# Message passing on a graph: 43 instead of 18 double groups of edges brought column by column or row by row, on ScalarE, VectorE and SyncE

## The chip, the cores and the metric

The kernel runs on one core of a Trainium2 chip. The metric is the device time of one execution in microseconds (us), lower is better; a median of several executions is compared. The core's engines each run their own instructions in order: TensorE (PE in the profile; its weight loads are PEld), VectorE (DVE), ScalarE (ACT), GpSimd (POOL) and SyncE (SP). They wait for each other through semaphores.

## The reference, cut to what matters

There are 12,500 nodes with 128 features, and 400,000 edges sorted by their target `dst`. Each edge has a random source `src` and 32 attributes.

```
h = max(layernorm(x), 0)
m = relu(concat(h[src], h[dst], edge_attr) @ w1 + b1) @ w2 + b2   # 288 -> 128 -> 128
agg = segment_sum(m, dst, 12500)
gi, gh = agg @ w_ih + b_ih, h @ w_hh + b_hh
r, z = sigmoid(i_r + h_r), sigmoid(i_z + h_z);  n = tanh(i_n + r * h_n)
out = x + (1 - z) * n + z * h
```

The part that cannot be a plain matrix product is `h[src]`: for every edge, the row of a random node.

## The kernel before

**Tables.** A first part normalises all nodes. It keeps `h` transposed in SBUF (`hT_all`, 128 features by 12,500 nodes, L60) and writes `A = h @ w1[0:128]` to DRAM (L118, L319), one row of 512 bytes for each node. So what an edge needs of its source is either the row `A[src]`, or the column `hT_all[:, src]`, which TensorE then multiplies by `w1a`.

**Tiling.** 128 edges are a tile and 8 tiles a double group (`PAIR`), 1,024 edges; there are 391 double groups (`NP`), numbered k. A double group is worked off in two units u = 2k and u = 2k+1 of four tiles each.

**The usual way of a double group.** GpSimd issues 8 indirect DMAs (`gather`, L135 to L146), each fetching 128 rows of `A` into a buffer `G`. There are `GBUFS` = 8 such buffers of 4 KB per partition, and 4 more that are in use only at the beginning (`EARLY`; the first ten double groups gather raw `x` rows, as `A` isn't ready yet). TensorE makes the other part of the layer in PSUM (`pre`, L582): a one-hot of the targets and the edge attributes, `L`, times `RW`, whose upper rows are the window's node rows. VectorE adds `G` (`add`, L605), ScalarE applies the ReLU (`relu`, L617), and TensorE sums the result by target with a second one-hot `OH` (`seg`, L625). VectorE takes the sums from PSUM (`take`, L638, whose count column ScalarE casts).

**By hand.** 18 double groups, listed in `order` (L83 to L91), aren't gathered. `one_by_one` (L762) copies, for each of the 1,024 edges, one column of `hT_all` (128 partitions by 4 bytes) into a tile `HE`: ScalarE by a copy (L775) for 10 double groups, VectorE by a `tensor_reduce` over one element (L777) for 8. The place of the column is in a register. 32 of them are loaded at a time by a register load (`LOAD`, L768), from a row of the tile `at`, which a DMA (L759) filled with node numbers and L880 turned into byte places. For such a double group `pre` adds 8 products with `w1a` (L601), `add` does nothing, and `relu` reads PSUM.

**The order of the work.** The program is written out by hand: Tile's scheduler is off (L58), and each engine takes its instructions in the order in which the loop over u (L862) issues them. In unit u stand, in this order: the requests of gathers whose buffer is coming free (`gathers`, L814); on even u, for every second double group, the loads of `L` and `Ld` on SyncE (`fetch`, L477: three DMAs); `run_jobs(u, 0)`; on even u `take(k-1)`; `stages(u)`; `run_jobs(u, 1)`, and on even u `window(k+3)` (VectorE copies 64 columns to `hw`, TensorE multiplies them, `oh`); `run_jobs(u, 2)`; `seg(u)`; `run_jobs(u, 3)`, and on even u `window_rows(k+3)` (VectorE adds `b1b` to `oh`, L524); a step of the node update. `stages(u)` holds on even u the one-hots for double group k+3 (`onehot_T` L489, `onehot` L526), then `pre(u+3)`, `add(u+2)`, `relu(u+2)`.

`run_jobs` (L795) spreads each by-hand job evenly over its units and their four phases, in steps of 4 edges. Jobs begin at unit 2*`JOBS0` = 32; a job ends 4 units before its double group's first unit, and the next of the same engine begins there. For 14 double groups at a time a `node` block (L646) does the gated update: a burst of small products on TensorE (L665, L670), carried over by VectorE (L650, L652), then four gates, each a step of its own, and the result to DRAM (L725).

GpSimd runs ahead of the others as far as free buffers let it; SyncE as far as `L`'s three buffers let it: a `fetch` stands in the program 2 units ahead of the use of what it loads, and its buffer was given back 4 units before it.

Of the kernel before, what the change touches and what calls it, by code (L numbers as in the profile page):

```python
# [8 lines left out]
F32 = mybir.dt.float32  # L9
F16 = mybir.dt.float16  # L10
I32 = mybir.dt.int32
U8 = mybir.dt.uint8
BF16 = mybir.dt.bfloat16
ET = mybir.EngineType
AF = mybir.ActivationFunctionType
ALU = mybir.AluOpType
AX = mybir.AxisListType

N, E, D, DE = 12500, 400000, 128, 32
T = E // 128  # L20

GRP = 4
PAIR = 2 * GRP
# [14 lines left out]
NFULL = N // 128  # L38
BAT = (4,) + (8,) * 11 + (NFULL - 92, 1)
RAW = 10  # L40
GBUFS = 8
EARLY = 4
PLACE = 20
CH = PLACE * PAIR
LOAD = 32
STEP = {"act": 4, "dve": 4}
SPREAD = {"act": 10, "dve": 8}
NR = 12672

H_AT = 16512  # L50
HOLD = -2


@with_exitstack
def tile_gnn(ctx: ExitStack, tc: tile.TileContext, x, src, srcT, dstT, dstP, eaT, eaP, w1, b1, w2T, b2,
             wih, bih, whh, bhh, out):
    nc = tc.nc
    ctx.enter_context(tc.manual_schedule())  # L58
    const = ctx.enter_context(tc.tile_pool(name="const", bufs=1))
    hT_all = const.tile([128, N], F32, name="hT_all")  # L60
    h_bytes = hT_all.bitcast(U8)
    gp = ctx.enter_context(tc.tile_pool(name="gp", bufs=GBUFS))
    p2 = ctx.enter_context(tc.tile_pool(name="p2", bufs=2))
# [7 lines left out]
    def tiles(k):  # L71
        return (0 if k == 0 else SUP0 + (k - 1) * PAIR, SUP0 + k * PAIR)
# [7 lines left out]

    JOBS0 = 2 * EARLY + GBUFS

    mode, order = {}, {m: [] for m in SPREAD}  # L83
    for m, n in SPREAD.items():
        lo = JOBS0 + 15
        for i in range(n):
            k = lo + int((i + 0.5) * (NP - 2 - lo) / n)
# [30 lines left out]
    A = dram.tile([N, D], F32, name="A")  # L118
# [3 lines left out]
    G = {}  # L122

    def early_pair(k):
        return k < EARLY or EARLY + GBUFS <= k < 2 * EARLY + GBUFS

    taker, rings = {}, {True: [], False: []}
    for k in range(NP):
        if k not in mode:
            ring = rings[early_pair(k)]  # L130
            size = EARLY if early_pair(k) else GBUFS
            taker[k] = ring[-size] if len(ring) >= size else -1
# [75 lines left out]
    with tc.tile_pool(name="pp", bufs=3) as pp:  # L208
# [50 lines left out]
        rows = const.tile([1, 6 * D + D], F32, name="rows")  # L259
# [18 lines left out]
        def chunk(q):  # L278
            b, c = chunks[q]
            i0, n = bats[b]  # L280
            return b, i0, c, min(n, c + 4), PB(b), (i0 + c) * 128
# [3 lines left out]
        for q in range(NC + 3):  # L285
            if q < NC:
                b, i0, c, e, P, n0 = chunk(q)
# [3 lines left out]
            if 1 <= q <= NC:  # L291
                b, i0, c, e, P, n0 = chunk(q - 1)
# [6 lines left out]
            if q >= 3:  # L299
                b, i0, c, e, P, n0 = chunk(q - 3)  # L300
# [4 lines left out]
            if q < NC:  # L305
                b, i0, c, e, P, n0 = chunk(q)
# [4 lines left out]
            if 1 <= q <= NC:  # L311
                b, i0, c, e, P, n0 = chunk(q - 1)
# [3 lines left out]
            if q >= 3:  # L316
                b, i0, c, e, P, n0 = chunk(q - 3)
                if e == bats[b][1]:
                    nc.sync.dma_start(nodes(A, i0, e, P), asb[b][:P, :e, :])  # L319
            if 2 <= q <= NC + 1:  # L320
                b, i0, c, e, P, n0 = chunk(q - 2)
                pas[q - 2] = ps2.tile([128, GRP, D], F32, name="pre")
                for j in range(c, e):
                    nc.tensor.matmul(pas[q - 2][:P, j - c, :], columns(b, j, j + 1)[:, 0, :],
                                     w1a, start=True, stop=True)
        for b0, b1, n in ((0, 1, BAT[0]), (1, 12, 8), (12, 13, BAT[12])):
            i0 = sum(BAT[:b0])
            for b in range(b0, b1):
                i = i0 + (b - b0) * n
# [32 lines left out]
    for a in range(2):  # L362
        s = slice(V * a, V * (a + 1))
        nc.vector.tensor_scalar(node_of[s, :], base_b[s, :, a], place_c[s, :], float(-V * a),
                                op0=ALU.add, op1=ALU.add)
# [109 lines left out]
    hand = {}  # L475
# [13 lines left out]
    def onehot_T(k):  # L489
        if k >= NP:  # L490
            return
        c = slice((k % QP) * 512, (k % QP + 1) * 512)
        nc.vector.tensor_scalar(Ls[k // QP][:2 * V, c], Ds[k // QP][:, c], node_of[:, k:k + 1],  # L493
                                None, op0=ALU.is_equal)
# [31 lines left out]
    def onehot(k):  # L526
        if k >= NP:
            return
        t0, t1 = tiles(k)
        OH[k] = OHB[k % len(OHB)]  # L530
        for a in range(2) if k == 0 else (None,):
            if a is None:
                o, s = OH[k].rearrange("p j a v -> p a j v"), slice(t0, t1)
                d = dloc[:, s].rearrange("p (a j) -> p a j", a=2)[:, :, :, None]
                shape = [128, 2, GRP, V]
                i = iota[:, None, None, :]
            else:
                e = min(t1, (a + 1) * GRP)
                o, d = OH[k][:, :e - a * GRP, a, :], dloc[:, a * GRP:e, None]
                shape = [128, e - a * GRP, V]  # L540
                i = iota[:, None, :]
            nc.vector.tensor_tensor(o, d.to_broadcast(shape), i.to_broadcast(shape),  # L542
                                    op=ALU.is_equal)
# [9 lines left out]
    def raw_h(u):  # L553
        if u < 2 * RAW:
            for i, s in enumerate(slots(u)):
                relu_norm(unit(u)[:, s, :], unit(u)[:, s, :], HE[u][:, i, :])

    def raw_stats(u):
        if u < 2 * RAW:
            l = slots(u)  # L560
            HE[u] = bn_sqrt(p2, bn(p2, lambda j: unit(u)[:, l[j], :], 128, len(l)), 128, len(l))

    def raw_fin(u):
        if u < 2 * RAW:
            n = len(slots(u))
            st = p2.tile([128, GRP, 2], F32, name="st_raw", bufs=4)
            bn_fin(p2, st[:, :n, :], HE[u], 128, n)
            HE[u] = st

    def raw_turn(u):  # L570
        if u < 2 * RAW:
            l = slots(u)
            pt = ps1.tile([128, 512], F32, name="misc")
            for i, s in enumerate(l):
                nc.tensor.transpose(pt[:, i * 128:(i + 1) * 128], unit(u)[:, s, :], ident)
            hT = p3.tile([128, 512], F32, name="hTe", bufs=2)
            nc.vector.tensor_copy(hT[:, :len(l) * 128], pt[:, :len(l) * 128])
            HE[u] = hT
# [171 lines left out]

    pj = []
    late = ExitStack()
    by_hand = order["act"] + order["dve"]
    NJ = len(by_hand)
    at = const.tile([NJ, PAIR * 128], I32, name="at")

    def job_indices(r):
# [2 lines left out]
            "(o e) -> o e", o=1))  # L760

    def one_by_one(m, k):  # L762
        et = {"act": ET.Activation, "dve": ET.DVE}[m]
        r = by_hand.index(k)
        hand[k] = pj[0].tile([128, PAIR * 128], F32, name=f"HE_{m}")
        he = hand[k].bitcast(U8)
        for e0 in range(0, PAIR * 128, LOAD):
            _, vals = nc.values_load_multi_w_load_instructions(  # L768
                at[r:r + 1, e0:e0 + LOAD], engines=[et], min_val=H_AT,
                max_val=H_AT + 4 * (N - 1),  # L770
                skip_runtime_bounds_check_because="src holds numbers of nodes")
            for i, v in enumerate(vals):
                e = e0 + i
                if m == "act":
                    nc.scalar.copy(he[:, e * 4:e * 4 + 4], h_bytes[:, bass.ds(v - H_AT, 4)])  # L775
                else:
                    nc.vector.tensor_reduce(he[:, e * 4:e * 4 + 4],  # L777
                                            h_bytes[:, bass.ds(v - H_AT, 4), None],
                                            AX.X, ALU.max)
                if i % STEP[m] == STEP[m] - 1:  # L780
                    yield

# [2 lines left out]
    for m, kl in order.items():  # L785
        start = 2 * JOBS0
        for k in kl:
            end = 2 * k - 4
            jobs.setdefault(start, []).append((m, k, end - start))
            start = end  # L790
    live = {}

    PH = 4
# [1 line left out]
    def run_jobs(u, phase):  # L795
# [3 lines left out]
        if phase == 0:  # L799
            for m, k, span in jobs.get(u, ()):  # L800
                live[m] = [one_by_one(m, k), u, span, PAIR * 128 // STEP[m], 0]
        for m, job in list(live.items()):
# [28 lines left out]
    def stages(u):  # L831
        if u + 7 >= 0:
            raw_stats(u + 7)
        if u + 6 >= 0:
            raw_fin(u + 6)
            raw_h(u + 6)
        if u % 2 == 0:
            onehot_T(u // 2 + 3)
            onehot(u // 2 + 3)
        if u + 4 >= 0:  # L840
            raw_turn(u + 4)
        if u + 3 >= 0:
            pre(u + 3)
        if u + 2 >= 0:
            add(u + 2)
            relu(u + 2)
# [15 lines left out]
    for u in range(NU):  # L862
        k, h = divmod(u, 2)
        gathers(u)
        if h == 0:
            if k % QP == 0:
                fetch(k // QP + 2)
            if k % BP == 0 and k:
                nodes_left.append([node(k // BP - 1), 0])
            if k % PLACE == 1:  # L870
                indices(k // PLACE + 2)
            if k % PLACE == 5:
                place(k // PLACE + 1)
                dst_tile(k // PLACE + 2)
            if k == NP - 20:
                check_windows()
        for r in range(2 * u, min(2 * u + 2, NJ)):
            job_indices(r)
        if u == 2 * JOBS0 - 2:
            nc.vector.tensor_scalar(at, at, 4.0, float(H_AT), op0=ALU.mult, op1=ALU.add)  # L880

        def other(phase):
            run_jobs(u, phase)
            if h == 0 and phase == 1:
                window(k + 3)
            if h == 0 and phase == 3:
                window_rows(k + 3)
            if phase == 3:
                step(nodes_left)

        other(0)
        if h == 0:
            take(k - 1)
        stages(u)
        other(1)
        other(2)
        seg(u)
        if u == 0:
            node_setup()
        other(3)  # L900
# [105 lines left out]
    f = nc.values_load(flag[0:1, 0:1], min_val=0, max_val=1)  # L1006
# [67 lines left out]
```

## Time and profile before

| | us |
|---|---|
| median of 3 runs (3842.6 to 3846.54) | 3845.28 |
| the profiled execution, whole | 3851.33 |
| its span, first to last instruction | 3849.6 |
| POOL busy in the span | 2895.7 (75%) |
| PE busy | 2660.6 (69%) |
| DVE busy | 2007.8 (52%) |
| ACT busy | 1650.1 (43%) |

In the profile an instruction is named by its line, its engine and the tiles that it writes and reads (`G<-A,src_i`). Of a group of like instructions the page gives the number, the time busy, the mean of one in ns, and the idle time of the engine just ahead of them with what ended it: another engine's instruction, a DMA that landed, or "issue", where the engine waited for nothing that the profile shows. Register loads aren't counted as busy; their time shows as idle time that "issue" ended. "SPq" is SyncE's instruction stream. PEclk is the clock granted to TensorE, as a share of full speed. A view of windows gives the busy time of the engines, and the number of instructions, in a stretch of the span.

### The profile page before, as it was taken

What the parts mean: (1) busy time and instruction counts of PE and PEld (TensorE: products, weight loads), DVE (VectorE), ACT (ScalarE), POOL (GpSimd) and SP (SyncE); (2) the same over time, 40 slices, a digit from 0 to 9 for tenths busy, and PEclk for the clock granted to TensorE, in tenths of its full rate; (3) what the DMA queues carried; (4) which work ended last, traced back from release to release, by engine and by line L of the source; (5) the groups of instructions that cost most, each with busy time, mean ns of one, the idle gap of its engine ahead of it and who ended that gap; (6) DMA issues with size and microseconds to landing.
All of it is one profiled execution on the core that took longest, in us unless ns stands there. A gap on an engine that the chain in (4) does not pass through costs nothing. (4 is left out here: it accounts for less than half of the span.)

```text
span 3849.6 us, 62154 instructions
## 1 busy us (share of the span) xinstructions
PE 2660.6 (69%) x13274; PEld 1624.1 (42%) x13274; DVE 2007.8 (52%) x12309; ACT 1650.1 (43%) x11720; POOL 2895.7 (75%) x2989
## 2 busy tenths in 40 slices
PE   6688766766775675776777577666667766775776
PEld 6554443443443443443444344433434443443443
DVE  7766655544545444554555455455545545544432
ACT  5446544444444444443544444444444444444311
POOL 7777777777777777777777777777777777777774
PEclk9888777777777777776777787687867777777776
DMA  6343333333333333333333333333333333333331
GB/s 202 87 99 93 85 91 84 77 87 82 88 82 87 82 84 85 84 86 79 90 84 83 81 88 87 77 92 78 89 80 89 77 87 82 89 80 85 88 81 38
DMA packets 151695, 333.68 MB, mean 87 GB/s; under 512 B 62088, under 2 KB 68019, under 8 KB 151317
## 3 DMA queue, kind: packets, MB, share of 16 engines
q0 software_dynamic: 95392, 195.55, 20.1%
q1 hardware_dynamic: 55781, 134.06, 13.5%
q8 instruction: 110, 1.80, 0.2%
q14 instruction: 268, 2.20, 0.2%
q10 hardware_dynamic: 144, 0.07, 0.0%
HBM read 315.60 MB, written 13.84 MB: 86 GB/s over the span
## 5 line engine op out<-in xcount | busy, mean ns | idle before, releaser
L144 POOL DMA_INDIRECT G<-A,src_i x2904 | 2821.9, 972 | 886.8 <-issue 837.3
L590 PE MATMUL pre<-RW,L 128*128 128x256 f32 x3128 | 1164.7, 505 | 120.4 <-DVE G L615 107.5
L775 ACT COPY HE_act<-hT_all 128x4 uint8 x10240 | 1055.5, 188 | 380.8 <-issue 378.9
L621 ACT ACTIVATE RB<-G 128x512 f32<-128x512 f32 x726 | 456.9, 629 | 1409.2 <-DVE G L615 1099.0
L615 DVE TENSOR_TENSOR G<-pre,G 128x512 f32<-128x512 f32 x726 | 499.8, 688 | 890.4 <-DMA G<-A,src_i 876.2
L515 PE MATMUL oh<-w1b,hw 128*64 128x128 f32 x782 | 217.1, 370 | 1019.8 <-DVE hw L512 1014.0
L590 PEld LDWEIGHTS pre<-RW,L 128*128 128x128 f32 x3128 | 696.7, 246 | 435.2 <-issue 311.3
L777 DVE TENSOR_REDUCE HE_dve<-hT_all 128x4 uint8 x8192 | 641.3, 148 | 359.8 <-issue 354.2
L634 PE MATMUL seg<-RB,OH 128*32 128x129 f32 x6250 | 657.4, 346 | 6.0 <-ACT dcol L643 4.4
L515 PEld LDWEIGHTS oh<-w1b,hw 128*64 128x64 f32 x782 | 92.6, 168 | 1184.2 <-DVE hw L512 1154.0
L634 PEld LDWEIGHTS seg<-RB,OH 128*32 128x32 f32 x6250 | 356.3, 133 | 256.6 <-issue 139.9
L524 DVE TENSOR_TENSOR RW<-oh,b1b 32x128 f32<-32x128 f32 x782 | 218.9, 280 | 171.8 <-PE oh L515 164.8
L642 DVE COPY sums<-seg 64x128 f32<-64x128 f32 x391 | 108.5, 278 | 211.0 <-PE seg L634 207.1
L493 DVE TENSOR_SCALAR L<-Ld,node_of 64x512 f32<-64x512 int32 x391 | 193.9, 496 | 0.1
L643 ACT CAST dcol<-seg 64x1 f16<-64x1 f32 x391 | 59.6, 152 | 261.2 <-DVE sums L642 259.0
L665 PEld LDWEIGHTS nd<-spot,sums 64*128 64x128 f32 x782 | 164.4, 321 | 13.8 <-issue 13.8
L665 PE MATMUL nd<-spot,sums 64*128 64x40 f32 x782 | 168.5, 404 | 0.0
L542 DVE TENSOR_TENSOR OH<-dloc,iota 128x256 f32<-128x256 f16 (+1 forms) x392 | 160.0, 408 | 0.0
L629 PE MATMUL seg<-zrow 1*64 1x129 bf16 x391 | 107.1, 274 | 0.0
L512 DVE COPY hw<-hT_all 128x64 f32 x391 | 85.3, 218 | 18.2 <-issue 7.0
L144 POOL DMA_INDIRECT G<-in_x,src_i x77 | 72.8, 946 | 24.9 <-issue 22.8
L629 PEld LDWEIGHTS <-zrow 1*64 1x64 bf16 x391 | 43.6, 111 | 97.4 <-issue 97.4
(147 smaller groups left out, 1366.4 us busy)
## 6 DMA issues: line engine op xcount, KB each, us to landing
L<-in_eaP SPq DMA_DIRECT2D x195, 256.0 KB
Ld<-in_dstP SPq DMA_DIRECT2D x390, 128.0 KB
G<-A,src_i POOLq DMA_INDIRECT x2904
xb<-in_x SPq DMA_DIRECT2D x28, 256.0 KB
out<-xb SPq DMA_DIRECT2D x28, 256.0 KB
xs<-in_x SPq DMA_DIRECT2D x11, 512.0 KB
A<-asb SPq DMA_DIRECT2D x11, 512.0 KB
src_i<-in_srcT SPq DMA_DIRECT2D x19, 80.0 KB
```

Source lines behind the costliest of these rows:

```text
L144: nc.gpsimd.indirect_dma_start(out=G[k][:, j, a, :], out_offset=None, in_=table, in_offset=bass.IndirectOffsetOnAxis(ap=src_i[c][:, i:i + ...
L493: nc.vector.tensor_scalar(Ls[k // QP][:2 * V, c], Ds[k // QP][:, c], node_of[:, k:k + 1], None, op0=ALU.is_equal)
L515: nc.tensor.matmul(PB_[k][:2 * V, :D], hw.rearrange("p a v -> p (a v)"), w1b, start=True, stop=True)
L524: nc.vector.tensor_tensor(RW[k % 4][s, a, :], pm[s, :D], b1b[s, :], op=ALU.add)
L542: nc.vector.tensor_tensor(o, d.to_broadcast(shape), i.to_broadcast(shape), op=ALU.is_equal)
L590: nc.tensor.matmul(PP[u][:, 2 * i:2 * i + 2, :], Ls[k // QP][:, c0:c0 + 128], RW[k % 4], start=True, stop=not raw)
L615: nc.vector.tensor_tensor(RT[u], PP.pop(u), RT[u], op=ALU.add)
L621: nc.scalar.activation(o[:, :, :D], RT.pop(u), AF.Relu)
L634: nc.tensor.matmul(SEG[k][V * a:V * (a + 1), :D + 1], OH[k][:, j, a, :], RB[u % 3][:, (j % 2) * 2 + a, :D + 1], start=False, stop=all(b != ...
L665: nc.tensor.matmul(pt[:, bass.ds(offs[i], V + SHIFT)], sums[:, i, :], spot, start=False, stop=i == n - 1)
L775: nc.scalar.copy(he[:, e * 4:e * 4 + 4], h_bytes[:, bass.ds(v - H_AT, 4)])
L777: nc.vector.tensor_reduce(he[:, e * 4:e * 4 + 4], h_bytes[:, bass.ds(v - H_AT, 4), None], AX.X, ALU.max)
```

## The change

The number of by-hand double groups goes from 18 to 43: ScalarE 19, VectorE 18, and SyncE, which had none, 6. Their places become k = 39, 40, 58, 59, 60, 77, 79, ... , 359, 360, 361, 379, 380: ScalarE's every 18 or 19, VectorE's every 20, SyncE's every 60.

SyncE's jobs are of another kind. For each edge SyncE issues one DMA of a row of `A`, 512 bytes, from DRAM into its row of one buffer `G_sp` (one buffer, 4 KB per partition). Such a double group is then handled as a gathered one: VectorE adds it. The place in `A` comes from a register. SyncE's steps are of 2 edges; its job ends 8 units ahead of its double group, and the next begins 2 units after it.

`GBUFS` goes from 8 to 7, and with it `JOBS0` from 16 to 15. `at` grows to 43 rows, of which SyncE's are multiplied by 512 and the others by 4. `onehot(k+3)`, which stood in the even unit behind `onehot_T(k+3)`, stands in the odd unit.

```diff
-GBUFS = 8
+GBUFS = 7
...
-STEP = {"act": 4, "dve": 4}
-SPREAD = {"act": 10, "dve": 8}
+STEP = {"act": 4, "dve": 4, "sp": 2}
+SPREAD = {"act": 19, "dve": 18, "sp": 6}
...
+ROW = 512
...
-    by_hand = order["act"] + order["dve"]
+    by_hand = [k for m in ("sp", "act", "dve") for k in order[m]]
     NJ = len(by_hand)
+    NSP = len(order["sp"])
+
+    place_of = const.tile([NJ, 2], F32, name="place_of")
+    for i, (to_sp, to_others) in enumerate(((ROW, 4), (0, H_AT))):
+        nc.vector.memset(place_of[:, i:i + 1], float(to_others))
+        nc.vector.memset(place_of[:NSP, i:i + 1], float(to_sp))
+    A_bytes = A.bitcast(U8).rearrange("n f -> (n f)")
...
-        et = {"act": ET.Activation, "dve": ET.DVE}[m]
+        et = {"act": ET.Activation, "dve": ET.DVE, "sp": ET.SP}[m]
         r = by_hand.index(k)
-        hand[k] = pj[0].tile([128, PAIR * 128], F32, name=f"HE_{m}")
-        he = hand[k].bitcast(U8)
+        if m == "sp":
+            G[k] = pj[0].tile([128, GRP, 2, D], F32, name="G_sp", bufs=1)
+            rows = G[k].bitcast(U8)
+        else:
+            hand[k] = pj[0].tile([128, PAIR * 128], F32, name=f"HE_{m}")
+            he = hand[k].bitcast(U8)
         for e0 in range(0, PAIR * 128, LOAD):
...
-                else:
+                elif m == "dve":
                     nc.vector.tensor_reduce(he[:, e * 4:e * 4 + 4],
                                             h_bytes[:, bass.ds(v - H_AT, 4), None],
                                             AX.X, ALU.max)
+                else:
+                    a, j = divmod(e // 128, GRP)
+                    nc.sync.dma_start(rows[e % 128:e % 128 + 1, j, a, :],
+                                      A_bytes[bass.ds(v, ROW)].rearrange("(o f) -> o f", o=1))
...
         for k in kl:
-            end = 2 * k - 4
+            end = 2 * k - (8 if m == "sp" else 4)
             jobs.setdefault(start, []).append((m, k, end - start))
-            start = end
+            start = end if m != "sp" else 2 * k + 2
...
         if u % 2 == 0:
             onehot_T(u // 2 + 3)
+        elif u > -7:
             onehot(u // 2 + 3)
...
-            nc.vector.tensor_scalar(at, at, 4.0, float(H_AT), op0=ALU.mult, op1=ALU.add)
+            nc.vector.tensor_scalar(at, at, place_of[:, 0:1], place_of[:, 1:2],
+                                    op0=ALU.mult, op1=ALU.add)
```

More of the change, by code (lines that the diff above doesn't have):

```diff
@@ L762, in one_by_one @@
     def one_by_one(m, k):
-        et = {"act": ET.Activation, "dve": ET.DVE}[m]
+        et = {"act": ET.Activation, "dve": ET.DVE, "sp": ET.SP}[m]
         r = by_hand.index(k)
-        hand[k] = pj[0].tile([128, PAIR * 128], F32, name=f"HE_{m}")
-        he = hand[k].bitcast(U8)
+        if m == "sp":
[4 more added lines that the diff above has]
+            he = hand[k].bitcast(U8)
         for e0 in range(0, PAIR * 128, LOAD):
+            low, high = (0, ROW * (N - 1)) if m == "sp" else (H_AT, H_AT + 4 * (N - 1))
             _, vals = nc.values_load_multi_w_load_instructions(
-                at[r:r + 1, e0:e0 + LOAD], engines=[et], min_val=H_AT,
-                max_val=H_AT + 4 * (N - 1),
+                at[r:r + 1, e0:e0 + LOAD], engines=[et], min_val=low, max_val=high,
                 skip_runtime_bounds_check_because="src holds numbers of nodes")
```

## The prediction

> **What bounds the kernel now.** I read the page's costliest groups first, then the windows, then VectorE's groups in the stretch from 500 to 3500 us, where all stages run, then timelines. On the page GpSimd's gathers stand alone: nothing else has so little idle time that another engine ended.
>
> ```profile
> L144 POOL DMA_INDIRECT G<-A,src_i x2904 | 2821.9, 972 | 886.8 <-issue 837.3
> L775 ACT COPY HE_act<-hT_all 128x4 uint8 x10240 | 1055.5, 188 | 380.8 <-issue 378.9
> L615 DVE TENSOR_TENSOR G<-pre,G 128x512 f32<-128x512 f32 x726 | 499.8, 688 | 890.4 <-DMA G<-A,src_i 876.2
> L777 DVE TENSOR_REDUCE HE_dve<-hT_all 128x4 uint8 x8192 | 641.3, 148 | 359.8 <-issue 354.2
> ```
>
> POOL's 2821.9 + 886.8 = 3708.7 us for 2904 gathers are 1.277 us each, and 837 of the 887 us idle are its own issue. VectorE's adds wait 876 us for rows to land, so VectorE, and ScalarE behind it, follow GpSimd's pace. What VectorE would need if rows were never late is in its groups of 500 to 3500 us:
>
> ```profile
> L777 DVE TENSOR_REDUCE HE_dve<-hT_all 128x4 uint8 x7111 | 558.0, 148 | 320.4 <-issue 316.6
> L615 DVE TENSOR_TENSOR G<-pre,G 128x512 f32<-128x512 f32 x588 | 405.0, 689 | 757.5 <-DMA G<-A,src_i 746.5 <-issue 5.9 <-ACT dcol L643 1.3
> L524 DVE TENSOR_TENSOR RW<-oh,b1b 32x128 f32<-32x128 f32 x618 | 172.9, 280 | 126.2 <-PE oh L515 120.8
> L642 DVE COPY sums<-seg 64x128 f32<-64x128 f32 x310 | 85.9, 277 | 149.4 <-PE seg L634 146.2 <-PE pre L601 2.6
> L512 DVE COPY hw<-hT_all 128x64 f32 x309 | 67.1, 217 | 14.8 <-DVE HE_dve L777 6.5 <-issue 4.3 <-DVE G L615 4.0
> L650 DVE TENSOR_TENSOR TOT<-nd,TOT 128x192 f32<-128x192 f32 x22 | 7.9, 358 | 86.0 <-PE nd L665 86.0
> ```
>
> 309 copies to `hw` are 309 double groups. Of the 3000 us 746.5 are waits for rows and 365 waits for PE (120.8, 148.8, 86.0 and some 9 more); 1888 are VectorE's own.
>
> **GpSimd's part.** 25 double groups more are not gathered: 200 gathers by 1.277 us, 255 us, so GpSimd alone would end at 3849.6 - 255 = 3594 us. Does its pace hold when VectorE is fuller?
>
> ```profile
> 3000.00:3500.00 500.00, 342.10 (x1678) 205.16 (x1679) 253.15 (x1615) 215.46 (x1609) 380.53 (x393) 0.75 0.33 84
> 3700.00:3800.00 100.00, 69.59 (x343) 41.04 (x342) 34.74 (x85) 15.29 (x33) 75.80 (x80) 0.77 0.27 71
> ```
>
> With VectorE 51% busy, 393 gathers take 500 us (1.272 each); once the by-hand jobs are over and VectorE is 35% busy, 80 take 100 us (1.25). If all of that 0.022 came from VectorE's share, a share of 95% would make 1.34, and 2781 gathers 3730 us. Counted in the trace, though, the gathers over 1 us are 287 of the 390 that lie beside a one-hot (L542), but 136 of the 1408 beside a by-hand reduce, near the 316 of all 2981. One-hots don't grow in number, reduces do; I take 1.277. The Trainium skill ("SBUF — State Buffer", section "Who interferes with whom") says of trn2 that a tensor_reduce never contends with GpSimd, while copies and tensor_scalars may lock it out: it agrees for the reduces, and not for the one-hots, which are tensor_tensors. Seven buffers for eight cost nothing while GpSimd is behind; when it isn't, they only shorten its lead by 10 us, once.
>
> **VectorE's part, the step that decides.** Reduces follow each other at 0.064 us (runs of 4, 8 and 12 last 0.34, 0.60 and 0.85 us), 65.5 us a job. A job has 32 register loads; 320.4 us of idle over 7111/32 = 222 loads are 1.44 each, and 1.25 in stretches where no rows were waited for (more is then still in the engine's queue). I take 1.35: 43 us. So a job costs 109 us (105 to 112). The rest: 1888 - 7111 x 0.064 - 317 = 1116 us over 309 double groups, 3.61 each; 19 fewer double groups to add, at 2 x 0.6 us, make it 3.54. With a job every 20 double groups VectorE's own work is 109/20 + 3.54 = 8.99 us per double group (8.8 to 9.15). GpSimd's between k = 39 and 380, with 298 of 341 gathered, is 8 x 1.277 x 298/341 = 8.93. The two meet; VectorE's waits for PE come on top.
>
> Today these are 365/309 = 1.18 us per double group, mostly after each node block's burst on PE:
>
> ```profile
> 1534.04 0.18 DVE L512 COPY hw<-hT_all 128x64 f32 x1
> ...
> 1542.91 0.36 DVE L650 TENSOR_TENSOR TOT<-nd,TOT 128x192 f32<-128x192 f32 x1 [5.63 <-PE nd L665]
> ...
> 1548.45 0.28 DVE L642 COPY sums<-seg 64x128 f32<-64x128 f32 x1 [3.30 <-PE seg L634]
> ```
>
> From the `hw` copy to L650 VectorE passes six phases. Each gets 51.2 - 23 = 28 more reduces an eighth, 0.23 us, and a share of loads (1.6 - 0.72)/8 x 1.35 = 0.15 us; with the one-hot of the odd half, 0.4, some 2.7 of the 5.6 us are filled. The 3.3 behind it hold 8 products with w1a (3.3 us on PE's timeline), which most blocks don't have. So 3 us remain for a block of 14, 0.2 each. From `hw` to L524 stand 12.8 reduces instead of 5.7, 0.8 us in place of most of a latency of 0.96; I leave 0.1. Outside the bursts the wait for `seg` goes: seven of eight phases, 2.7 us more work, lie ahead of it. Ends: 0 (all filled) and 1.18 (nothing filled). I take 0.3: **9.3 us per double group**.
>
> **ScalarE's part.** Its 8835 copies in the same stretch follow at 0.095 us with 330 us of load idle: 97 + 38 = 136 us a job; the rest is 1.5 us per double group. A job every 18.9: 136/18.9 + 1.5 = 8.7 us. That hides under VectorE's 9.3; a ReLU may come up to two units late (its use, `seg`, is two units on). Without that cover it would cost what exceeds 8.9, nothing.
>
> **SyncE's part.** 6144 row DMAs and 192 register loads on a queue that now mostly waits. No row shows such a DMA; the nearest are one-partition loads of 4 KB (L759):
>
> ```profile
> 132.15 0.48 SPq L483 DMA_DIRECT2D L<-in_eaP  x1
> 132.68 1.06 SPq L486 DMA_DIRECT2D Ld<-in_dstP  x2
> 133.78 3.75 SPq L759 DMA_DIRECT2D at<-in_src  x8
> 154.03 0.57 SPq L759 DMA_DIRECT2D at<-in_src  x2
> 154.65 0.35 SPq L111 DMA_DIRECT2D dst_i<-in_dstT  x1
> ```
>
> Two in a row take 0.31 each with the gap, eight 0.47, since an issue waits until the eighth before it has landed, here those of the fetch. Bounds 0.31 and 0.47; a place out of a register adds 0.04 (L656 with 0.37 against L229's 0.33). I take 0.33: rows of 512 bytes land sooner than the fetch's 256 KB. What is queued behind them: the fetches of `L` and `Ld` (1.6 us each, one every 4 units, used 2 units later), without which VectorE's L493 and PE stop. A job of 110 units has 110 x 4.6 = 506 us and may be late by the 6 units (27 us) a fetch has to spare: 533, less 32 loads of 2 us and 28 fetches, 60, leaves 0.40 us per row. The first has 82 units, some 428 us in all, and 0.313 per row: at 0.33 it costs 17 us, at 0.47 160 and the others 72 each. The Trainium skill ("DMA: Bandwidth & Descriptors", "Rules for kernel authors") speaks against these rows: below 64 KB a transfer pays mostly overhead, and its fit ("Anatomy of one DMA") gives 2 us each. By it, one at a time, 6144 would take an estimated 12.3 ms; eight in flight make 0.25 us each, below the rows above.
>
> The index loads for 25 rows more (0.3 us each, before unit 22) lie in SyncE's waits. PE's 152 products with w1a, 0.3 us, lie in its 860 us of waits for `hw` in the stretch.
>
> **The sum**, with the two ends of the trace as they are:
>
> ```profile
> 226.30 0.63 ACT L621 ACTIVATE RB<-G 128x512 f32<-128x512 f32 x1 [1.42 <-DMA G<-A,src_i]
> 3810.60 0.63 ACT L621 ACTIVATE RB<-G 128x512 f32<-128x512 f32 x1 [4.36 <-DVE G L615]
> ```
>
> The first is double group 15's: 226 us. To 39, 24 at 8.6 (the first job has 23 double groups: 109/23 + 3.6 + 0.3): 207. To 380, 341 x 9.3 = 3171. The last ten: jobs are over, GpSimd has some five still to gather, 5 x 10.2 = 51; from the last ReLU to the end 39, as now. SyncE's first job 15. Sum 3709 us of span; the median before is 4 us below the span, so **3705 us** (-3.6%).
>
> **The rivals.** (1) GpSimd stays the bound: VectorE's waits are all filled, 8.8 to 9.0 us per double group, and the end is 3594 to 3640. For it: the two rates are equal to 1%; against it: a burst of 9 us on PE can't be filled by 3. (2) Slower: SyncE becomes the bound. Place: the fetches behind the rows. From 0.40 us per row each job runs over; at 0.41 the sum of 15 becomes 100 + 5 x 10 = 150 and the gain is gone; at 0.47 it is 520 and the time 4210. For it: the run of eight; against it: half its time are waits for the fetch's landing. (3) Slower: PE's waits return in full, because PE's chain grows with VectorE's (TOT, gates and `oh` each wait for a VectorE result). At 9.0 + 1.18 = 10.2 us: 226 + 226 + 3478 + 105 = 4035 us; it decides from 9.7 on. Against it: PE waits 860 us for `hw` now. That the change doesn't do what it says is not one: the built program has 200 gathers fewer, 10240 reduces, 9216 copies and 6144 row DMAs more.
>
> **How the numbers follow.** The forecast, 3640 to 3790 us, has 0.53; rival 1 0.17; a mild SyncE or PE loss between 3790 and 3838 0.05; no change within 0.2% (about what a measurement of this kernel can tell) 0.03; rival 2 0.13; rival 3 0.09. Faster 0.75, same 0.03, slower 0.22. The range 3592 to 3862 leaves out most of the two slower ones.
>
> **What would show it.** After: 2704 gathers, POOL idle ended by ACT or DVE (a buffer) for some 100 us, and VectorE's wait for rows down from 876 to under 150 us; L777's successor with some 1.35 us per load; waits of L650 near 3 us. SP rows 0.3 to 0.36 apart and L493 never waiting for `Ld`. I am wrong if L493 waits for DMA (rival 2), or if the waits for PE stay near 1 us per double group (rival 3), or if POOL is idle only by its issue (rival 1).

## The result and the profile after

The changed kernel takes 3712.0 us (median of four runs, 3701.45 to 3715.73) against 3843.94 us before (3841.85 to 3846.54): a ratio of 0.9652, with a 95% interval of 0.9635 to 0.9668. The profiled execution took 3701.45 us, its span is 3699.7 us. 3705 had been forecast, so the time came out as said. Its parts didn't: two terms of the sum were wrong by 70 to 80 us each, with opposite signs, and the experiments found a version of 3599 us.

These are the costliest groups of the page, those that answer to the ones shown of before. All lines have moved: L144 is L146 now, L493 L495, L524 L526, L542 L544, L615 L617, L642 L644, L775 L788, L777 L790.

```profile
L146 POOL DMA_INDIRECT G<-A,src_i x2704 | 2589.9, 958 | 980.1 <-issue 770.2
L788 ACT COPY HE_act<-hT_all 128x4 uint8 x19456 | 1966.1, 189 | 583.2 <-issue 580.6
L790 DVE TENSOR_REDUCE HE_dve<-hT_all 128x4 uint8 x18432 | 1336.4, 146 | 716.0 <-issue 707.4
L617 DVE TENSOR_TENSOR G<-pre,G 128x512 f32<-128x512 f32 x676 | 461.0, 682 | 10.1 <-PE pre L592 0.3
L526 DVE TENSOR_TENSOR RW<-oh,b1b 32x128 f32<-32x128 f32 x782 | 217.7, 278 | 48.2 <-PE oh L517 39.8
L495 DVE TENSOR_SCALAR L<-Ld,node_of 64x512 f32<-64x512 int32 x391 | 192.4, 492 | 83.3 <-DMA Ld<-in_dstP 69.5
L644 DVE COPY sums<-seg 64x128 f32<-64x128 f32 x391 | 107.4, 275 | 73.2 <-PE seg L636 69.2
```

The adds (L617) have lost their waits for rows: 876 us before, 10.1 us of idle time in all now. Of GpSimd's 980 us idle, on the other hand, 770 are its own issue and 210 aren't; 837 of 887 were before. The view of waits of POOL says what the rest is:

```profile
POOL G L146 <- issue: 793.0, 2587, 4.6
POOL G L146 <- ACT RB L623: 156.6, 56, 31.2
```

The columns are the total in us, the times, the longest. GpSimd now waits for the ReLU that gives a buffer back, up to 31 us at a time: the bound has gone over to those who empty the buffers. New is the line of L495. It makes one-hots of targets out of `Ld`, which SyncE fetches, and waits 83 us. All of that lies in one stretch, 220 to 680 us, as the waits of VectorE in that stretch show:

```profile
DVE HE_dve L790 <- issue: 77.1, 62, 1.8
DVE L L495 <- DMA Ld<-in_dstP: 69.5, 14, 7.6
DVE L L495 <- DMA G_sp<-A: 13.8, 3, 9.0
DVE TOT L652 <- PE nd L667: 8.9, 3, 4.4
DVE sums L644 <- PE seg L636: 4.5, 3, 1.5
```

69.5 and 13.8 us, both of L495, which needs only the fetch: the rows of `G_sp` on the same queue are most likely named where one of them landed last. It is the stretch of SyncE's first job. Of SyncE's stream and VectorE's (start in us, duration, instruction):

```profile
299.91 1.20 SPq L795 DMA_DIRECT2D G_sp<-A  x4
301.37 0.40 SPq L727 DMA_DIRECT2D out<-xb  x1
301.86 0.49 SPq L485 DMA_DIRECT2D L<-in_eaP  x1
302.41 1.04 SPq L488 DMA_DIRECT2D Ld<-in_dstP  x2
303.56 22.67 SPq L795 DMA_DIRECT2D G_sp<-A  x50
326.34 0.48 SPq L485 DMA_DIRECT2D L<-in_eaP  x1
326.87 1.04 SPq L488 DMA_DIRECT2D Ld<-in_dstP  x2
```

```profile
308.15 0.48 DVE L495 TENSOR_SCALAR L<-Ld,node_of 64x512 f32<-64x512 int32 x1 [9.05 <-DMA G_sp<-A]
331.15 0.65 DVE L495 TENSOR_SCALAR L<-Ld,node_of 64x512 f32<-64x512 int32 x1 [6.53 <-DMA Ld<-in_dstP]
```

SyncE issues without a break. Between two fetches stand 50 rows, and it takes 24.5 us (301.86 to 326.34) for what is worth two double groups, 12.2 us each. L495 starts 3 to 5 us after the last instruction of the fetch, and VectorE has stood still for 9.05 and 6.53 us. VectorE, PE and in the end GpSimd go at SyncE's pace here.

Two stretches of the windows show the same in the busy times (PE, PEld, DVE, ACT, POOL, then clock, DMA share, GB/s):

```profile
500.00:1000.00 500.00, 340.48 (x1667) 205.57 (x1664) 338.02 (x3023) 328.17 (x2817) 329.57 (x346) 0.75 0.31 80
3000.00:3500.00 500.00, 365.85 (x1869) 222.63 (x1867) 370.31 (x3327) 367.05 (x3188) 376.03 (x394) 0.78 0.34 88
```

346 gathers in the first, 394 in the last, where VectorE at 370 us "busy" of 500 is full: its register loads are idle time in this view.

### The profile page after: what moved, and what is told of

Its sections match the earlier page's. It is cut to its first block, busy times and chain, and to the rows that moved or that the text cites. A ratio compares the mean times of both kernels' runs of the same rounds, so it can differ in the third digit from the quotient of the medians.

```text
span 3699.7 us, 94893 instructions
## 1 busy us (share of the span) xinstructions
PE 2649.8 (72%) x13578; PEld 1639.6 (44%) x13578; DVE 2627.5 (71%) x22515; ACT 2513.9 (68%) x20936; POOL 2663.7 (72%) x2789
## 5 line engine op out<-in xcount | busy, mean ns | idle before, releaser
L146 POOL DMA_INDIRECT G<-A,src_i x2704 | 2589.9, 958 | 980.1 <-issue 770.2
L788 ACT COPY HE_act<-hT_all 128x4 uint8 x19456 | 1966.1, 189 | 583.2 <-issue 580.6
L790 DVE TENSOR_REDUCE HE_dve<-hT_all 128x4 uint8 x18432 | 1336.4, 146 | 716.0 <-issue 707.4
L592 PE MATMUL pre<-RW,L 128*128 128x256 f32 x3128 | 1151.4, 497 | 129.8 <-DVE G L617 95.7
L592 PEld LDWEIGHTS pre<-RW,L 128*128 128x128 f32 x3128 | 685.8, 243 | 439.0 <-issue 287.0
L636 PE MATMUL seg<-RB,OH 128*32 128x129 f32 x6250 | 645.4, 341 | 0.0
L623 ACT ACTIVATE RB<-G 128x512 f32<-128x512 f32 x676 | 424.7, 628 | 323.2 <-DVE G L617 85.2
L617 DVE TENSOR_TENSOR G<-pre,G 128x512 f32<-128x512 f32 x676 | 461.0, 682 | 10.1 <-PE pre L592 0.3
L526 DVE TENSOR_TENSOR RW<-oh,b1b 32x128 f32<-32x128 f32 x782 | 217.7, 278 | 48.2 <-PE oh L517 39.8
L495 DVE TENSOR_SCALAR L<-Ld,node_of 64x512 f32<-64x512 int32 x391 | 192.4, 492 | 83.3 <-DMA Ld<-in_dstP 69.5
L544 DVE TENSOR_TENSOR OH<-dloc,iota 128x256 f32<-128x256 f16 (+1 forms) x392 | 162.4, 415 | 0.5 <-issue 0.2
L644 DVE COPY sums<-seg 64x128 f32<-64x128 f32 x391 | 107.4, 275 | 73.2 <-PE seg L636 69.2
L667 PEld LDWEIGHTS nd<-spot,sums 64*128 64x128 f32 x782 | 150.4, 296 | 13.1 <-issue 13.1
L667 PE MATMUL nd<-spot,sums 64*128 64x40 f32 x782 | 154.5, 381 | 0.0
L146 POOL DMA_INDIRECT G<-in_x,src_i x77 | 72.9, 946 | 24.9 <-issue 22.9
```

The costliest lines, as they stand in the source:

```text
L146: nc.gpsimd.indirect_dma_start(out=G[k][:, j, a, :], out_offset=None, in_=table, in_offset=bass.IndirectOffsetOnAxis(ap=src_i[c][:, i:i + ...
L526: nc.vector.tensor_tensor(RW[k % 4][s, a, :], pm[s, :D], b1b[s, :], op=ALU.add)
L592: nc.tensor.matmul(PP[u][:, 2 * i:2 * i + 2, :], Ls[k // QP][:, c0:c0 + 128], RW[k % 4], start=True, stop=not raw)
L617: nc.vector.tensor_tensor(RT[u], PP.pop(u), RT[u], op=ALU.add)
L623: nc.scalar.activation(o[:, :, :D], RT.pop(u), AF.Relu)
L636: nc.tensor.matmul(SEG[k][V * a:V * (a + 1), :D + 1], OH[k][:, j, a, :], RB[u % 3][:, (j % 2) * 2 + a, :D + 1], start=False, stop=all(b != ...
```

## The experiments

Each kernel below is the changed one with the edit shown, except where it says otherwise. The first four were timed on one chip, where the kernel before took 3844.02 us (3836.78 to 3846.93, seven runs).

**SyncE's double groups evenly, the first one later.** If SyncE's first job is short of time, more of it must bring the time back.

```diff
-            k = lo + int((i + 0.5) * (NP - 2 - lo) / n)
+            k = 75 + 60 * i if m == "sp" else lo + int((i + 0.5) * (NP - 2 - lo) / n)
```

> SyncE's six double groups moved to k = 75, 135, 195, 255, 315, 375, so that its first job has 112 units instead of 82 and the others 110; nothing else is changed. Theory A (SyncE's first job runs late and VectorE's L495 waits for Ld behind it, 83 us in the changed kernel between 220 and 680 us; the other jobs fit): those waits fall under 15 us, the time falls by 70 to 90 us to 3620 to 3645 us, where GpSimd's own 3594 us is near. Theory B (SyncE is full in every job, 500 us of some 506, and the loss only moves on): waits of L495 for DMA stay over 50 us in sum and the time falls by less than 30 us, to over 3680 us. Theory C (VectorE sets the pace of the early part too, and the wait is a sign, not the cause): no change within 10 us.

3623.31 us (3615.23 to 3625.7), a ratio of 0.942 (0.9403 to 0.9437), where the change alone has 0.9652: 89 us come back from one line. In its profile the groups of the gathers and of L495 read:

```profile
L146 POOL DMA_INDIRECT G<-A,src_i x2704 | 2587.4, 957 | 897.6 <-issue 781.2 <-ACT RB L623 75.1 <-DMA G<-A,src_i 17.4
L495 DVE TENSOR_SCALAR L<-Ld,node_of 64x512 f32<-64x512 int32 x391 | 191.6, 490 | 0.2 <-issue 0.2
```

L495's 83.3 us of idle time are 0.2. Between unit 30 and unit 112 (the end of SyncE's first job in the change) lie 453.4 us after and 361.6 here, 92 less. From there to unit 758 it is 2932.5 us after and 2945.9 here. So, though the edit moves all six jobs, the loss lies in the first. GpSimd still waits 75 us for buffers.

**No jobs for SyncE.** 37 double groups by hand; SyncE's six are gathered.

```diff
-SPREAD = {"act": 19, "dve": 18, "sp": 6}
+SPREAD = {"act": 19, "dve": 18}
...
-    by_hand = [k for m in ("sp", "act", "dve") for k in order[m]]
+    by_hand = [k for m in ("act", "dve") for k in order[m]]
...
-    NSP = len(order["sp"])
+    NSP = 0
...
-        nc.vector.memset(place_of[:NSP, i:i + 1], float(to_sp))
```

> SyncE's six double groups are gathered by GpSimd again; ScalarE 19, VectorE 18, seven buffers and the odd halves as in the changed kernel. Theory A (SyncE's jobs save GpSimd 48 gathers, 61 us, but cost some 83 us at their beginning): GpSimd alone needs 3594 + 61 = 3655 us, VectorE's own sum without the early waits is some 3610, so the time is 3655 to 3690 us, below the changed kernel's 3712, with GpSimd never waiting for ACT for long. Theory B (row DMAs are a gain as they stand): slower than the changed kernel, over 3725 us. If VectorE is the bound all through, without help from GpSimd's relief: 3620 to 3650 us.

3635.07 us (3631.05 to 3639.8), 0.9454 (0.9438 to 0.947). That is 77 us quicker than with SyncE's jobs where the change puts them, and 12 us slower than with them spread evenly: six double groups on SyncE are worth 12 us, placed as they were they cost 77. The time is 20 us and more below what the first theory expected. It lies where VectorE was to be the bound all through, but that isn't what the profile shows: GpSimd waits for buffers for 25.7 us only. It is the gathers that are quicker.

```profile
L146 POOL DMA_INDIRECT G<-A,src_i x2752 | 2637.2, 958 | 867.4 <-issue 798.5 <-ACT RB L623 25.7 <-DMA G<-A,src_i 18.6
```

(2637.2 + 867.4 - 25.7) / 2752 = 1.264 us for a gather with its own idle time, not the 1.277 of before, though VectorE is much fuller. Why, is the next question.

**The one-hot of places back in the even half.**

```diff
             onehot_T(u // 2 + 3)
-        elif u > -7:
             onehot(u // 2 + 3)
```

> The changed kernel with VectorE's one-hots of places (L544) back in the even half, behind onehot_T; all else as changed. Prediction's step: in the odd half the 0.4 us fill waits for PE, in the even half they lie between take and the copy to hw, on PE's chain. Theory A: the waits for seg and for the node bursts grow by 0.1 to 0.3 us per double group, and the time by 20 to 90 us (3730 to 3800). Theory B (the place is of no weight, since VectorE does the same work in either half and waits for PE 0.37 us per double group only): within 10 us of 3712.

3721.1 us (3715.01 to 3725.4), 0.9677 (0.9659 to 0.9695): 9 us above the change, with intervals that overlap. In the time there is next to nothing, as the second theory said. VectorE's waits for `seg` grow from 69.2 to 93.1 us and those of L652 from 65.1 to 73.4, less than 0.1 us per double group. In the gathers there is a lot.

```profile
L146 POOL DMA_INDIRECT G<-A,src_i x2704 | 2651.9, 981 | 937.3 <-issue 786.2 <-ACT RB L623 110.6 <-DMA G<-A,src_i 17.7
```

(2651.9 + 937.3 - 110.6) / 2704 = 1.286 us, against (2589.9 + 980.1 - 156.6) / 2704 = 1.262 with the move: 65 us of GpSimd's time. A timeline of this kernel, GpSimd and VectorE, shows one place where it goes:

```profile
2004.68 0.94 POOL L146 DMA_INDIRECT G<-A,src_i  x1 [0.30 <-issue]
2005.93 1.70 POOL L146 DMA_INDIRECT G<-A,src_i  x1 [0.30 <-issue]
2007.94 0.94 POOL L146 DMA_INDIRECT G<-A,src_i  x1 [0.30 <-issue]
```

```profile
2006.01 0.47 DVE L495 TENSOR_SCALAR L<-Ld,node_of 64x512 f32<-64x512 int32 x1
2006.40 0.41 DVE L544 TENSOR_TENSOR OH<-dloc,iota 128x256 f32<-128x256 f16 x1
```

The gather that L495 and the one-hot of places (L544) fall on, one directly behind the other, takes 1.70 us instead of 0.94. After, L544 stands 5 us behind L495, and a gather beside L495 takes 1.02:

```profile
2002.21 1.02 POOL L146 DMA_INDIRECT G<-A,src_i  x1 [0.30 <-issue]
```

```profile
2002.64 0.47 DVE L495 TENSOR_SCALAR L<-Ld,node_of 64x512 f32<-64x512 int32 x1
2007.87 0.41 DVE L544 TENSOR_TENSOR OH<-dloc,iota 128x256 f32<-128x256 f16 x1
```

Counted over the whole traces, with the time above 0.944 us summed over all gathers:

| kernel | gathers over 1 us | time above 0.944 us | long of those beside L544 | beside L495 | beside a by-hand reduce |
|---|---|---|---|---|---|
| before | 316 of 2981 | 83 us | 287 of 390 | 181 of 445 | 136 of 1408 |
| one-hot back | 297 of 2781 | 102 us | 278 of 384 | 186 of 412 | 226 of 2041 |
| the change | 204 of 2781 | 40 us | 59 of 394 | 134 of 430 | 149 of 2006 |
| SyncE evenly | 192 of 2781 | 38 us | 74 of 417 | 102 of 416 | 141 of 2070 |

So it is above all the pair, and not the reduces: in the change, of 1367 gathers beside a reduce and neither of the two others, 5 are long. Nor is it only a matter of where in the gather the two happen to fall. Where L495 starts in the first 0.2 us of a gather, the 54 gathers of the change take at most 0.003 us more than 0.944, and where the one-hot alone starts 0.4 to 0.6 us into it, so do 51; with the pair at that place, 55 gathers take 0.405 us more on the mean. Why the pair holds a gather up to 0.82 us, about its own length of 0.80 us, where at that place each alone costs nothing, can't be read from these traces. The gain in GpSimd's pace hardly shows in the time here, because VectorE and SyncE set it: where its gathers take 65 us more, 46 us of its waits for buffers are gone (110.6 for 156.6).

**Less for VectorE.** With SyncE's jobs even, what is left of GpSimd's waits is VectorE. So the first edit again, and

```diff
-SPREAD = {"act": 19, "dve": 18, "sp": 6}
+SPREAD = {"act": 19, "dve": 15, "sp": 6}
```

> As e1_sp_even, but VectorE has 15 by-hand double groups instead of 18, 40 in all: 24 more gathers. Theory A (VectorE's queue is the bound of e1 after the first job, at some 9.1 us per double group against GpSimd's 8.93): VectorE's own work falls by 109 x (1/20 - 1/24) = 0.9 us per double group, GpSimd becomes the only bound at 3594 + 31 = 3625 us, so the time is 3625 to 3650, VectorE waits for gathered rows (over 100 us in sum), GpSimd's waits for ACT are under 20 us. Rival (TensorE's chain or ScalarE sets the pace): GpSimd still waits for buffers for 100 us or more, and the time is that of e1 or less than it by more than 20 us.

3598.65 us (3596.29 to 3603.61), 0.9361 (0.9345 to 0.9376): three double groups fewer by hand, and 25 us quicker than with 18. It beats both kernels. The signs are those of the first theory, and the time is below what it expected, again by the gathers' pace.

```profile
L146 POOL DMA_INDIRECT G<-A,src_i x2728 | 2617.6, 960 | 843.6 <-issue 789.3 <-DMA G<-A,src_i 21.6 <-PE misc L577 12.5
L617 DVE TENSOR_TENSOR G<-pre,G 128x512 f32<-128x512 f32 x682 | 466.4, 684 | 196.8 <-DMA G<-A,src_i 173.6 <-issue 7.4 <-ACT dcol L645 5.7
```

```profile
POOL G L146 <- ACT RB L623: 10.1, 33, 0.3
```

GpSimd no longer waits for buffers (10.1 us, never longer than the 0.3 us of its own issue), and VectorE waits 173.6 us for rows. GpSimd alone sets the end: 3849.6 - 176 x 1.277 = 3625 us of span would be its old pace, 3601.4 is measured.

**Runs that could not be compared.** Eight further kernel runs, four and four, fell on two other chips (on record as 3 and 7, the first four experiments as 0), on both of which the kernel before itself takes 5369 us. Their ratios can't be carried over, since other things bound the kernel there. The kernel before with only the one-hot of places moved was meant to show what the move brings where GpSimd sets the time:

```diff
         if u % 2 == 0:
             onehot_T(u // 2 + 3)
+        elif u > -7:
             onehot(u // 2 + 3)
```

> The kernel before with one edit alone: VectorE's one-hots of places (L542) in the odd half. Of its 2981 gathers 316 take over 1 us, and the time above 0.944 us sums to 83 us; 287 of the 390 gathers beside a one-hot are among them. In the changed kernel, with the one-hots in the odd half, the sum is 40 us. Theory A (the one-hot right behind the one-hot of targets, L493, holds gathers up; apart they don't): GpSimd is the bound of the kernel before, so its time falls by those 43 us, to 3795 to 3810 us, and under 100 of the gathers beside one-hots are long. Theory B (the prediction's: a one-hot costs a gather the same wherever it stands, so the move only changes VectorE's order): within 8 us of the kernel before. Theory C (GpSimd is quicker in the changed kernel because VectorE is fuller with reduces): the sum stays at 83 us.

> The kernel before with one edit alone: VectorE's one-hots of places (L542) in the odd half, on a chip on which the kernel before takes some 3844 us. Of its 2981 gathers 316 take over 1 us, and the time above 0.944 us sums to 83 us; 287 of the 390 gathers beside a one-hot are among them. In the changed kernel the sum is 40 us. Theory A (the one-hot right behind the one-hot of targets, L493, holds gathers up; apart they don't): GpSimd is the bound of the kernel before, so its time falls by those 43 us, to 3795 to 3810 us, and under 100 of the gathers beside one-hots are long. Theory B (the prediction's: a one-hot costs a gather the same wherever it stands): within 8 us of the kernel before. Theory C (GpSimd is quicker in the changed kernel because VectorE is fuller with reduces): the sum stays at 83 us.

5407.22 us, a ratio of 1.006 (1.0029 to 1.009), and 5395.04, 1.0047 (1.0011 to 1.0083). In the second's profile GpSimd doesn't set the time at all: of its 2474 us idle 1501.5 are waits for the ReLU, where the usual chip has next to none in the kernel before. VectorE waits 1958 us ahead of the copy that takes the sums (L642), 211 before on the usual chip, and most of it is put down to "remote": what ended the wait isn't among the instructions that the profile shows.

```profile
L144 POOL DMA_INDIRECT G<-A,src_i x2904 | 2771.3, 954 | 2474.2 <-ACT RB L621 1501.5 <-issue 851.6 <-DMA stats<-st_all 68.5
L642 DVE COPY sums<-seg 64x128 f32<-64x128 f32 x391 | 109.9, 281 | 1958.0 <-remote 1618.6 <-PE seg L634 164.6 <-issue 126.9
```

In some stretches ScalarE's copies have half a microsecond ahead of each in which nothing was awaited (over 0.3 us ahead of 823 of the 10,240 copies, 317 before on the usual chip):

```profile
2058.27 0.19 ACT L775 COPY HE_act<-hT_all 128x4 uint8 x1 [0.52 <-issue]
2058.96 0.19 ACT L775 COPY HE_act<-hT_all 128x4 uint8 x1 [0.50 <-issue]
2059.67 0.20 ACT L775 COPY HE_act<-hT_all 128x4 uint8 x1 [0.52 <-issue]
```

So the experiment didn't test its question in the time: what the move alone is worth where GpSimd sets the time stays open. Its gathers agree with what was seen above (142 and 137 of 2981 over 1 us, and 32 and 31 us above 0.944), but there is no profile of the kernel before on these chips to set beside them. Why these chips are slower stays open.

The other three there were variants of the even version: `"dve": 16`, `"dve": 21`, and `GBUFS = 6` (with `JOBS0` kept by writing `2 * EARLY + 7`), each twice.

> As e4_even_dve15 with 16 VectorE jobs in place of 15 (41 by hand). Theory A (GpSimd is the only bound there, at 1.264 us a gather): 8 gathers fewer are 10 us, so 3585 to 3596 us. Rival (VectorE comes in again): the same as e4 or up to 15 us more.

> As e4_even_dve15 with 16 VectorE jobs in place of 15 (41 by hand), on a chip on which the kernel before takes some 3844 us. Theory A (GpSimd is the only bound there, at 1.264 us a gather): 8 gathers fewer are 10 us, so 3585 to 3596 us. Rival (VectorE comes in again): the same as e4 or up to 15 us more.

> As e1_sp_even with 21 VectorE jobs in place of 18 (46 by hand). Theory A (VectorE's queue is the bound from 18 on, 109 us a job): three jobs more are 327 us of VectorE's work, less 4 us of adds, of which some 50 us go into waits for PE that are left: 3860 to 3950 us, slower than the kernel before or level with it, with GpSimd waiting for ACT for over 250 us. Rival (GpSimd or a chain through PE is the bound of e1, VectorE has room): 24 gathers fewer, 3590 to 3640 us.

> As e1_sp_even with 21 VectorE jobs in place of 18 (46 by hand), on a chip on which the kernel before takes some 3844 us. Theory A (VectorE's queue is the bound from 18 on, 109 us a job): three jobs more are 327 us of VectorE's work, less 4 us of adds, of which some 50 us go into waits for PE that are left: 3860 to 3950 us, slower than the kernel before or level with it, with GpSimd waiting for ACT for over 250 us. Rival (GpSimd or a chain through PE is the bound of e1, VectorE has room): 24 gathers fewer, 3590 to 3640 us.

> As e1_sp_even with 6 buffers for gathered rows in place of 7; jobs begin at the same unit. Theory A (a buffer is worth only a shorter lead of GpSimd, which matters where VectorE falls behind): 0 to 15 us more than e1's 3623. Rival (with VectorE and GpSimd level, each buffer counts, and the step from 8 to 7 cost the changed kernel too): over 25 us more.

> As e1_sp_even with 6 buffers for gathered rows in place of 7; jobs begin at the same unit; on a chip on which the kernel before takes some 3844 us. Theory A (a buffer is worth only a shorter lead of GpSimd, which matters where VectorE falls behind): 0 to 15 us more than e1's 3623. Rival (with VectorE and GpSimd level, each buffer counts, and the step from 8 to 7 cost the changed kernel too): over 25 us more.

| | us | ratio to before there |
|---|---|---|
| 16 on VectorE | 5373.82 and 5364.96 | 1.0011 (0.9979 to 1.0044), 1.0005 (0.9975 to 1.0035) |
| 21 on VectorE | 5729.0 and 5724.18 | 1.0656 (1.0606 to 1.0705), 1.0679 (1.0617 to 1.074) |
| six buffers | 5514.52 and 5506.37 | 1.0245 (1.0198 to 1.0292), 1.0265 (1.0205 to 1.0325) |

Against each other they say one thing: on these chips, five more jobs on VectorE cost 355 and 359 us, some 71 us each. What the slope is on the usual chip, what a buffer is worth, and whether 16 or 17 jobs would beat 15, stays open: the even version with 18 wasn't run there, nor these on the usual chip.

## Why the prediction came out, step by step

The forecast of 3705 us was only 7 us off, and that is luck: two errors cancelled. These are the terms of its sum beside the profile of the change, by the starts of the ReLUs of the same double groups:

| term | predicted | measured |
|---|---|---|
| to double group 15 | 226 | 223 |
| 15 to 39 | 207 | 256 |
| 39 to 380 | 3171 | 3139 |
| the last ten | 51 | 54 |
| from the last ReLU to the end | 39 | 28 |
| SyncE's first job | 15 | 92 (against SyncE evenly), within "15 to 39" and "39 to 380" |
| sum | 3709 | 3700 |

**What failed: "at 0.33 it costs 17 us".** The price of a row was right: the rows start 0.323 us apart (median), inside the 0.30 to 0.36 named as the sign. This is the view of them in the change:

```profile
L795 SPq MOVE G_sp<-A x6144: 29/29/38, 224.3 to 3410.4; - x199
L795 SPq DMA_DIRECT2D G_sp<-A x6144: 224/228/470, 224.3 to 3410.5; - x199
```

228 ns of issue, 29 ns for the register's move, the rest gaps. (The 2 us that the prediction names from the Trainium skill are stated in that section for DMAs that GpSimd issues, and these are SyncE's.) What was wrong is, first, the time that the job had. "The first has 82 units, some 428 us in all" is 10.4 us for a double group, or 9.8 if the 27 us of a fetch's slack are in it. But the same sum goes through these 41 double groups at 8.6 (24 of them) and 9.3 (17), 365 us, which with the slack makes 392. That was right: in the version where SyncE isn't in the way, the 82 units take 361.6, and 389 with the slack. The rows of the early double groups are in part there already when their turn comes: before, the 24 of 15 to 39 took 182 us, 7.6 each, less than their gathers.

Second, the job took more than its rows at 0.33. It ran for 467 us (224.3 to 691.1): 357 for the rows, 17.5 of these waiting for the fetch's loads to land, 68 for register loads of 2.2 each, some 35 for the fetches and 7 for the rest. 467 - 389 = 78 us late, near the 83 that L495 waited. Of these 78, 17 had been forecast; 39 are time that the job didn't have, 17.5 are the waits for landing, which the price of 0.33 left out, and 4 are register loads. The other five jobs take 489 to 501 us from the first row to the last, of the 506 that they were given, and L495 doesn't wait behind them, as said, though there is little to spare.

**Rival 2 therefore happened, in one job of six**, in the place named (L495 waiting for `Ld`), at a row price at which it was to cost 17 us. Of the two signs for SyncE one came true (0.30 to 0.36) and one didn't (L495 never waiting for `Ld`), and that one the prediction had named as a sign of being wrong.

**VectorE's pace: "9.3 us per double group".** Behind SyncE's first job, from unit 112 to 758, the change needs (3609.2 - 676.7) / 323 = 9.08 us. 716.0 us of idle over 576 register loads are 1.24 each, the lower bound, not the 1.35 taken: 0.11 x 32 / 20 = 0.18 us per double group. The waits for PE were sized well: the groups of VectorE from 500 to 3400 us, 314 double groups,

```profile
L526 DVE TENSOR_TENSOR RW<-oh,b1b 32x128 f32<-32x128 f32 x628 | 174.7, 278 | 21.4 <-PE oh L517 14.3
L644 DVE COPY sums<-seg 64x128 f32<-64x128 f32 x314 | 86.1, 274 | 48.9 <-PE seg L636 47.8
...
L652 DVE TENSOR_TENSOR TOT<-nd,TOT 128x192 f32<-128x192 f32 x23 | 8.2, 356 | 49.6 <-PE nd L667 49.4
```

give 14.3 + 47.8 + 49.4 and 4 more, 116 us or 0.37 each (0.3 said, 1.18 before), and 49.6 / 23 = 2.2 us for a node block (3 said). That sum makes 9.2 us, and 9.08 came; a tenth is unaccounted for. The 0.22 below 9.3, over 323 double groups, are 71 us, which paid for most of SyncE's first job.

**GpSimd's pace: "I take 1.277".** With the one-hot back in the even half it is 1.286, so beside the fuller VectorE it did get worse, by 0.009 us a gather or 24 us in all, far less than the 1.34 that the prediction named as the worst. The move of the one-hot then took it to 1.262, because it parts it from the tensor_scalar. The prediction had the count that showed it (287 of 390 beside the one-hot) and read it as a matter of the one-hot's number, when its neighbour was being changed: the move was costed as 0.4 us of filling for VectorE's waits. It is worth 65 us of GpSimd's time, 40 against the pace before. In the change this is hidden behind VectorE. In the version with 15 jobs, which lies 24 us below the 3625 of the old pace, it most likely shows; that is argued from the gathers, as no run has the 15 jobs with the one-hot in the even half.

The prediction also said that the Trainium skill ("SBUF — State Buffer", "Who interferes with whom") didn't agree for the one-hots. The same section says that a VectorE instruction with two inputs in SBUF contends with a GpSimd instruction that reads SBUF, and the one-hot is one of these (the gather reads its row numbers, `src_i`, in SBUF). With that the runs agree: in the change, a gather takes 0.17 us longer on the mean where a one-hot alone starts up to 0.2 us ahead of it (44 of them), and 0.18 us where a tensor_scalar alone does (66). The section also reports a probe in which a tensor_tensor didn't stall a DMA; that these runs don't show. That the pair holds a gather for so long, the page doesn't say.

**Rival 1**, GpSimd alone at 3594 to 3640 us, isn't what the change does: GpSimd waits 156.6 us for buffers, "some 100" said. But it is what the change could have been, 3599 us, with SyncE's first job given more time and with three jobs fewer on VectorE. **Rival 3** didn't happen: the waits for PE are 0.37 us per double group. That **ScalarE** stays hidden and that the eighth buffer costs nothing was argued and no run here tests it alone: the version at GpSimd's own pace has both, with 19 jobs on ScalarE and seven buffers.

## What to carry to other kernels

Work given to an in-order queue delays what stands behind it, so its budget has to be made stage by stage, with the pace at which that stage will run after the change, the one that the forecast itself uses for it elsewhere; a job that fits five times out of six sets the time by the sixth. Where work is shared out between engines until they are equal, less is more: the last three by-hand double groups on VectorE cost 25 us, as they took it past GpSimd. And where an instruction is moved out of the way of a second one, look who else was held up by the two together.

## What the runs showed of the hardware

- A gather takes 0.94 us of GpSimd and up to 1.76 where a tensor_scalar (0.47 us, int32 to f32) and a tensor_tensor with two inputs in SBUF (0.41 us) follow each other directly on VectorE: 278 of 384 gathers beside the one-hot are then over 1 us, 59 of 394 if the two are some 5 us apart and the tensor_scalar is mostly followed by the add, which reads PSUM. By-hand reduces do no such harm (5 of the 1367 gathers that have only reduces of these three beside them).
- DMAs of one row of 512 bytes, with the place from a register, go out 0.323 us apart on one queue, 228 ns of issue and 29 ns of move each. A register load of 32 values costs SyncE 2.2 us and VectorE 1.24 us of idle time.
- On two chips the kernel before ran 1.4 times as long (5369 us on both, for 3844). With only the one-hot moved, VectorE waits 1958 us there ahead of the copy of the sums, 1618.6 of them for something that the profile doesn't show.
